# A decoder block in f32: the norm's sums of squares taken from turned x by one-column products, and a product moved ahead

## The chip, the cores and the metric

The kernel runs on one core of one Trainium2 chip. The metric is the device time of one execution in microseconds (us); the times of the kernel before are 1396.84, 1398.39 and 1398.48, median 1398.39. All arithmetic is f32. Each core has five engines that run side by side and meet through semaphores: PE (TensorE, matmuls; PEld is its weight load), DVE (VectorE), ACT (ScalarE), POOL (GpSimd), and SP, which here issues every transfer.

## The reference

A decoder block over x of shape (16, 256, 512), 4096 tokens of 512 channels. It has three parts, each with a residual and a layer norm behind it. What matters here is the beginning of the first:

```
xn   = x * rsqrt(mean(x*x, axis=-1) + EPS) * w_norm
proj = einsum('bld,td->blt', xn, W_in)          # z, xi, dt, B, C
xi   = silu(causal_conv4(xi))
...                                             # a scan over time with dA, u, C
y    = einsum('blh,ih->bli', y, W_h2i) * silu(z)
out  = einsum('bli,di->bld', y, W_out) + residual
x    = layernorm(x + out)
...                                             # long convolution with skip, contraction
...                                             # feed-forward with gated LoRA experts
```

## The kernel before, in words

The first part works on 8 groups of 512 tokens (`GT`), the other two on 32 slices of 8 time steps. The order of instructions on every engine is the order in which the program writes them; nothing is reordered by a scheduler, so a product that waits holds up all products behind it.

For a group the kernel needs x twice. `xnT` holds it turned, channels on partitions: four chunks `kc` of 128 channels by 512 tokens, which is what the projections multiply. `xt` holds it with tokens on partitions, four tiles of 128 tokens by 512 channels; it is the residual, added at the end of the group (L855). In the kernel before, the `xt` tiles also give the norm. `rms` (L404) squares each tile with an accumulated sum along the row (ACT L415, DVE L411), adds the epsilon (L417) and takes the power -1/2 on POOL (L419). That gives one number for each token, on partitions. `along_tokens` (L422) turns such numbers into rows that are equal on all partitions, by a product with the identity (L425), and `normed` (L444) multiplies `xnT` by them and by the norm's weight `wn` (L446). For the first group `rms` and `along_tokens` run in two halves of 256 tokens. Later groups take their rows through DRAM.

The projections use a scheme with seven products in place of eight for a block of 2 by 2 (`Xs`): four blocks of the turned x ("11", "12", "21", "22"), four sums of blocks `T1` to `T4` (L251, L254, L255, L257), and for each pair of weight blocks four weight sums `S1` to `S4` (`weight_sums`, L261 to L264, on POOL). A call of `product` (L356) is two matmuls of 256 columns. `begin_products` makes the block product A11 by "11", `first_products` three more: S1 by `T1`, S2 by `T2`, S3 by `T3`; the last three follow one step later. For the very first pair of the first group the second pair's `begin_products` is put between its T1 and T2 products, through the argument `between`:

```
if between is not None:
    between()
product(al[:, S:], w, p, S2, "T2", stop=True)
product(be[:, S:], w, p, S3, "T3", stop=True)
```

TensorE also multiplies the identity by itself at the start, for no result: `idle(n)` (L517) issues n such products of 128 columns, eight at first (`WARM`), then four after each half of the norm.

Transfers are issued by SP in program order. At the start these are: the four tiles `xt` (256 KB each), `wn`, the first half of `xnT` (512 KB), the first pair of `w_xi`, the second half of `xnT`, further weights (512 KB for a pair), small vectors, the rest of `w_z`, `w_bc`, then `w_h` and `w_o`. A transfer can wait until the one eight places before it has landed.

Of the kernel before, what the change touches and what calls it, by code (L numbers as in the profile page):

```python
# [8 lines left out]
F32 = mybir.dt.float32  # L9
# [5 lines left out]
P = 128  # L15
# [58 lines left out]
def decoder_kernel(  # L74
# [135 lines left out]
    with ExitStack() as s1:  # L210
# [12 lines left out]
        def load_x(g):  # L223
            xs = []
            for t in range(TT):
                xt = xp.tile([P, D], F32, tag="xt", name="xt")
                nc.sync.dma_start(xt, xg[g * TT + t])
                xs.append(xt)
            return xs
# [34 lines left out]
            eng.tensor_tensor(w[:, p, S4], w[:, p, A12], w[:, p, S2], ALU.subtract)  # L264
            return ins

        xs_next = load_x(0)
        wn = wp.tile([P, KD], F32, name="wn")
        nc.sync.dma_start(wn, w_norm)
        w_xi = big.tile([P, NI // 2, 7, 2, P], F32, tag="big", name="w_xi")  # L270
        w_z = big.tile([P, NI // 2, 7, 2, P], F32, tag="big", name="w_z")
        nc.sync.dma_start(xnT[:, 0:2], xTg[:, 0:2, 0:GT])
        nc.sync.dma_start(w_xi[:, 0, 0:4], Wxi[:, 0])
        nc.sync.dma_start(xnT[:, 2:4], xTg[:, 2:4, 0:GT])
        nc.sync.dma_start(w_xi[:, 1, 0:4], Wxi[:, 1])
        nc.sync.dma_start(w_z[:, 0, 0:4], Wz[:, 0])
        for p in range(2, NI // 2):
# [11 lines left out]
            nc.sync.dma_start(w_z[:, p, 0:4], Wz[:, p])  # L289
        w_bc = w1.tile([P, 2, 7, 2, P], F32, name="w_bc")  # L290
        nc.sync.dma_start(w_bc[:, :, 0:4], Wbc)


        w_h = w1.tile([P, 2, 2, P], F32, name="w_h")
# [69 lines left out]
                    skip_group_check=upon,  # L364
                )

        def begin_products(w, p, third):

            al, be = [
                ps_s.tile([P, 512], F32, tag="s", name="s") if third else bank() for _ in range(2)  # L370
            ]
            product(al[:, 0:S], w, p, A11, "11", start=True)
            return al, be

        def first_products(w, p, third, begun=None, between=None):

            al, be = begun or begin_products(w, p, third)
            product(be[:, 0:S], w, p, S1, "T1", start=True)
            if between is not None:
                between()  # L380
            product(al[:, S:], w, p, S2, "T2", stop=True)
            product(be[:, S:], w, p, S3, "T3", stop=True)
            return al, be
# [17 lines left out]
            nc.vector.tensor_tensor(to[1], u, be[:, 0:S], ALU.add)  # L401
            nc.vector.tensor_tensor(to[2], u, be[:, S:], ALU.add)

        def rms(xs, both=False):  # L404

            n = len(xs)
            ss = p2.tile([P, TT], F32, tag="ss", name="ss")[:, 0:n]
            for t in range(n):
                sq = p2.tile([P, D], F32, tag="acc", name="sq", bufs=6)
                if both and t % 2:  # L410
                    nc.vector.scalar_tensor_tensor(  # L411
                        sq, xs[t], 1.0, xs[t], ALU.mult, ALU.mult, accum_out=ss[:, t : t + 1]
                    )
                else:
                    nc.scalar.activation(sq, xs[t], AF.Square, accum_out=ss[:, t : t + 1])  # L415
            ms = p2.tile([P, TT], F32, tag="ms", name="ms")[:, 0:n]
            nc.vector.tensor_scalar(ms, ss, 1.0 / D, RMS_EPS, ALU.mult, ALU.add)  # L417
            rstd = p2.tile([P, TT], F32, tag="rstd", name="rstd")[:, 0:n]
            nc.gpsimd.tensor_tensor(rstd, ms, nhalf[:, 0:n], ALU.pow)  # L419
            return rstd  # L420

        def along_tokens(ps, rstd):  # L422

            for t in range(2):
                nc.tensor.matmul(  # L425
                    ps[:, t * P : (t + 1) * P],
                    rstd[:, t : t + 1].to_broadcast([P, P]),
                    ident,
                    start=True,
                    stop=True,  # L430
                )
# [85 lines left out]
        def idle(n):  # L517

            ps = bank()
            for _ in range(n):  # L520
                nc.tensor.matmul(ps[:, 0:P], ident, ident, start=True, stop=True)


        rt = ps_t.tile([P, GT], F32, tag="tr", name="rt")
        idle(WARM)
        for b in range(GB):
            along_tokens(
                rt[:, b * S : (b + 1) * S], rms(xs_next[b * TT // GB : (b + 1) * TT // GB], True)
            )
            idle(WARM // 2)  # L530
        normed(rt, (0, 1))
        first_token_sum(nc.vector)
        normed(rt, (2, 3))
# [54 lines left out]
        for g in range(groups):  # L588
# [97 lines left out]
            for i, (kind, p) in enumerate(order):  # L686
                if g == 1 and i == 2:
                    with_identity(w_f)
                if g in (2, 3) and i == 5:
                    w, cols = ((w_f, D), (w_gl, NG))[g - 2]  # L690
                    sums.append((w, cols, chunk_sum(w, cols)))
                if i == 6:
                    ms = [head_means(0)]
                if g == 0 and i == 0:
                    al, be = first_products(
                        kinds[kind], p, True, None,
                        lambda: begun.append(begin_products(w_xi, order[1][1], False)),
                    )
                else:
                    al, be = first_products(  # L700
                        kinds[kind], p, i % 3 == 0, begun.pop(0) if begun else None
                    )
                if i == 8:
                    ms.append(head_means(1))
                if i == 9:


                    yps = ps_t.tile([P, S], F32, tag="tr", name="yps")
                    for ht in range(HT):
                        for b in range(GB):  # L710
                            nc.tensor.matmul(
                                yps[b * HP : (b + 1) * HP],
                                sel[:, ht].rearrange("p q h -> p (q h)"),
                                Bs[ht][:, b * S : (b + 1) * S],
                                start=(ht == 0),
                                stop=(ht == HT - 1),
                            )
                    if sums:
                        centred(*sums.pop(0))
                if before is not None:  # L720
                    finish_products()
                to = places(kind, p)
                u = first_sums(al, be, to)
                if i == 8:
                    states(1, stepped(ms[1], spreads[2]), spreads[3])
                if i == 6:
                    ms = [stepped(ms[0], spreads[0])]
                    spreads.append(spread(1, 1))
                if g == 0:
                    if i == 1:  # L730
                        parts = decays()
                    if i == 2:
                        nc.scalar.activation(A, A, AF.Exp)
                        nc.vector.tensor_scalar(A, A, -1.0, None, ALU.mult)
                    if i in (1, 2, 4):
                        next(parts)
                if i == 9:
                    yT = q3.tile([P, S], F32, tag="vn", name="yT", bufs=1)
                    nc.scalar.copy(yT, yps)
                if before is not None:  # L740
                    finish_sums((lambda: next(parts)) if g == 0 and i == 2 else None)
                if g == 0 and i == 3:
                    next(parts)
                if g == 0 and i in later:
                    for n, (w, k) in enumerate(later[i]):
                        ins = weight_sums(nc.gpsimd, w, k)
                        if n == 0:
                            wait_for(ins, mixes[-1])
                if i == 7:
                    states(0, ms[0], spreads[1])  # L750
                if i == 8:
                    outputs(0)
                    outputs(1)
                    if more:
                        rt = to_dram(rms(xs_next))
                    if g == 0:
                        behind = []
                        w_sums = w_o_sums(behind)
                        next(w_sums)
                before = (kind, p, al, be, u, to)  # L760
                if g:
                    if i in (2, 5):
                        for one in turning[:2]:
                            turned(g - 1, *one)
                        del turning[:2]
                    if i in (0, 2):
                        t, r = late[i // 2]
                        late[i // 2] = t, r, spreads_of(r)
                    if i in (1, 3):
                        normalised(g - 1, *late[i // 2])  # L770
                        turning.append(late[i // 2][:2])
                if i == (6 if g else 1) and more:
                    xs_next = load_x(g + 1)
# [995 lines left out]
```

## Time and profile before

| | |
|---|---|
| median of three runs | 1398.39 us |
| profiled execution | 1399.62 us |
| its span, first to last instruction | 1397.8 us |
| PE busy | 1379.8 us, 99% of the span |
| DVE busy | 1186.5 us, 85% |
| POOL busy | 620.2 us, 44% |
| ACT busy | 450.2 us, 32% |

The profile is of one execution. The sections show busy time by engine, the span in slices, the chain of work that ended last, and groups of instructions; a line as L425 is a line of the kernel before. A f32 matmul appears as two records, each with its weight load. In a timeline a row is start, length, engine, line, operation, output and inputs, the number of records merged, and in brackets the idle time ahead of it with what ended it. Busy time of TensorE counts records, which overlap, so it is not a measure of how much of its peak is used.

### The profile page before, as it was taken

The numbers are of one execution on the slowest core, as the hardware profiler recorded it, in microseconds if no ns is written. First come the engines' busy times: TensorE is split into PE (matmuls) and PEld (weight loads), VectorE is DVE, ScalarE is ACT, GpSimd is POOL, SyncE is SP. The second block draws the span as 40 slices with busy tenths as digits, with TensorE's granted clock in tenths as the row PEclk, the third lists the DMA queues.
The fourth block names the chain that finished last, engine by engine and source line by source line (L and its number), as shares of the span: only waits on it lengthen the run. The fifth ranks groups of instructions, "written<-read, shape, count | busy, mean of one in ns | idle before, by whom it ended". The sixth has DMA issues, their size and how long they took to land.

```text
span 1397.8 us, 19582 instructions
## 1 busy us (share of the span) xinstructions
PE 1379.8 (99%) x6967; PEld 935.3 (67%) x6967; DVE 1186.5 (85%) x2270; ACT 450.2 (32%) x979; POOL 620.2 (44%) x849
## 2 busy tenths in 40 slices
PE   8999999999999999999999999999999999999997
PEld 7888788788888887888886345445454454545444
DVE  6888879878788787788866889999999999999986
ACT  2524324243243342432421323333323333333232
POOL 5451021020100201001003768877888788887884
PEclk9999999999999999999999999999999999999999
DMA  8113212212113131121306554454543555345500
GB/s 307 34 38 91 63 54 37 69 40 55 39 41 68 49 68 39 41 53 42 80 20 87 69 69 64 60 74 61 76 64 60 74 76 76 61 61 72 65 27 38
DMA packets 362386, 89.48 MB, mean 64 GB/s; under 512 B 330032, under 2 KB 334512, under 8 KB 362288
## 3 DMA queue, kind: packets, MB, share of 16 engines
q1 hardware_dynamic: 362288, 88.23, 34.1%
q8 instruction: 55, 0.90, 0.3%
q14 instruction: 43, 0.35, 0.1%
HBM read 70.62 MB, written 17.58 MB: 63 GB/s over the span
## 4 chain that ended last, share of the span: by engine, by line
PE 94%; DVE 3%; issue 1%; DMA 1%; POOL 0%; ACT 0%; SPq 0%; POOLq 0%; DVEq 0%
PE mm L358 21%; PE y L1088 15%; PE s L358 14%; PE y L1103 12%; PE s L826 6%; PE mm L826 6%; PE y L1070 4%; PE be L1335 4%; PE al L1335 3%; PE gl L1280 2%; PE xm L634 1%; PE mm L783 1%; PE mm L920 1%; PE al L1307 1%; PE s L920 1%
## 5 line engine op out<-in xcount | busy, mean ns | idle before, releaser
L1136 DVE TENSOR_TENSOR pr<-y,cT 128x1024 f32<-128x1024 f32 x126 | 148.4, 1219 | 38.4 <-PE y L1103 37.7
L1103 PE MATMUL y<-kv 64*64 64x512 f32 x1536 | 179.6, 598 | 0.0
L187 DVE TENSOR_TENSOR kv<-tr,cT 128x1024 f32<-128x1024 f32 x128 | 150.0, 1212 | 0.8 <-ACT tr L179 0.8
L623 DVE SCALAR_TENSOR_TENSOR acc<-xi,wc,acc 128x512 f32<-128x512 f32 x192 | 142.8, 757 | 7.4 <-ACT acc L619 1.8
L1146 DVE TENSOR_REDUCE red<-pr 128x128 f32<-128x1024 f32 x126 | 147.1, 1208 | 0.0
L1088 PE MATMUL y<-kv 128*128 128x512 f32 x272 | 128.3, 594 | 3.5 <-DVE pr L1136 3.4
L1103 PEld LDWEIGHTS y<-kv 64*64 64x64 f32 x1536 | 52.2, 132 | 118.6 <-issue 96.7
L69 POOL TENSOR_TENSOR rs_a<-ve_a,nhalf 128x1 f32<-128x1 f32 x32 | 17.5, 546 | 255.3 <-DVE ve_a L67 255.0
L1088 PE MATMUL y<-kv,Td 128*128 128x512 f32 x248 | 116.5, 592 | 0.0
L419 POOL TENSOR_TENSOR rstd<-ms,nhalf 128x4 f32<-128x4 f32 (+1 forms) x9 | 8.6, 954 | 229.7 <-DVE ms L417 229.7
L358 PE MATMUL mm<-XT,w_z 128*128 128x256 f32 x384 | 90.7, 379 | 0.0
L1088 PEld LDWEIGHTS y<-kv,Td 128*128 128x128 f32 x248 | 47.1, 190 | 59.3 <-issue 59.3
L1077 ACT COPY y<-y 64x512 f32<-64x512 f32 x120 | 67.0, 558 | 59.5 <-PE y L1070 57.6
L1088 PEld LDWEIGHTS y<-kv 128*128 128x128 f32 x272 | 51.1, 189 | 44.9 <-ACT y L1077 17.3
L1054 POOL TENSOR_TENSOR xs<-kv 128x512 f32<-128x512 f32 x63 | 80.2, 1273 | 0.1
L358 PEld LDWEIGHTS mm<-XT,w_z 128*128 128x128 f32 x384 | 73.0, 190 | 9.9
L358 PE MATMUL mm<-xnT,w_z 128*128 128x256 f32 x288 | 70.8, 382 | 0.0
L1490 POOL TENSOR_TENSOR ol<-o,red 128x512 f32<-128x512 f32 x31 | 39.3, 1267 | 61.4 <-DVE red L1146 61.4
L251 POOL TENSOR_TENSOR XT<-xnT 128x512 f32<-128x512 f32 x7 | 9.3, 1326 | 129.0 <-PE mm L826 129.0
L1070 PE MATMUL y<-xs,kv 128*128 128x512 f32 x120 | 62.2, 600 | 0.4
L358 PE MATMUL s<-XT,w_xi 128*128 128x256 f32 x256 | 61.0, 380 | 0.8 <-DVE XT L254 0.5
L358 PEld LDWEIGHTS mm<-xnT,w_z 128*128 128x128 f32 x288 | 54.0, 190 | 10.1 <-issue 3.0
(337 smaller groups left out, 3065.6 us busy)
## 6 DMA issues: line engine op xcount, KB each, us to landing
cT<-in_ctxT SPq DMA_DIRECT2D x32, 384.0 KB
kv<-in_toep SPq DMA_DIRECT2D x32, 384.0 KB
xt<-in_x SPq DMA_DIRECT2D x32, 256.0 KB
spread<-both SPq DMA_DIRECT2D x32, 256.0 KB
first<-xt SPq DMA_DIRECT2D x124, 64.0 KB
vT<-first SPq DMA_DIRECT2D x31, 256.0 KB
out<-res SPq DMA_DIRECT2D x31, 256.0 KB
xnT<-in_xT SPq DMA_DIRECT2D x7, 1024.0 KB
```

The costliest lines, as they stand in the source:

```text
L187: last = nc.vector.tensor_tensor(kv[:, q, k * BQ : (k + NL // 2) * BQ], vT[:, q, blks].rearrange("p k (b i) -> p (k b) i", i=NH).unsqueeze ...
L358: nc.tensor.matmul(ps, w[:, p, a, kc, :], Xs[b][:, kc, :], start=start and kc == 0, stop=stop and kc == 1, skip_group_check=upon,)
L623: ins = nc.vector.scalar_tensor_tensor(acc, xi[:, :, k : k + S], wc[:, c, k : k + 1], acc, ALU.mult, ALU.add)
L826: nc.tensor.matmul(ps, own[a][c][:, n * P : (n + 1) * P], w_o[b][c], start=start and c == 0, stop=stop and c == HC - 1, skip_group_check=upon,
L1054: return nc.gpsimd.tensor_tensor(xs[:, q], moving(kv, q, 0), moving(kv, q, 1), ALU.add)
L1070: nc.tensor.matmul(seed, T[:, SHARED_AT, :], xs[:, q], start=True, stop=True)
L1077: nc.scalar.copy(bank_of(y, 2)[b : b + HP], seed[a : a + HP])
L1088: nc.tensor.matmul(bank_of(y, lb), w, moving(kv, q, mb), start=not late and lb not in begun, stop=False, skip_group_check=True,)
L1103: return nc.tensor.matmul(bank_of(y, lb)[cols], T[rows, DIAGONAL_AT, (b - a) * HP : (b - a + 1) * HP], moving(kv, q, lb)[rows], start=star ...
L1136: nc.vector.tensor_tensor(pr.rearrange("p (k b j) i -> p k b j i", k=2, j=NH), y[i].rearrange("p k (b j i) -> p k b j i", j=NH, i=NH), cT[ ...
L1146: nc.vector.tensor_reduce(red[:, q, 2 * i : 2 * i + 2, :].rearrange("p k t -> p (k t)"), pr, AX.X, ALU.add)
L1335: nc.tensor.matmul(ps, a[:, kc, :], w[:, kc, :], start=(start and kc == 0), stop=(kc == 1), skip_group_check=True,)
```

## The change

Four things change, all in the first group.

The transfers: both halves of `xnT` are now issued first, then `wn`, then the weights as before; the four tiles `xt` of the first group are issued after `w_bc`, ahead of `w_h` and `w_o`.

The norm of the first group: a new function `rms_from_columns` squares the four chunks of `xnT` (two on ACT, two on DVE) and sums over channels on TensorE. For each chunk and each 128 tokens the squared block is the stationary operand and one column of -1/2 (`nhalf`) the moving one, sixteen products of one column, accumulated in one bank. `inverse`, the former end of `rms`, scales by -2/D. `idle(WARM // 4)`, two products, stands after chunks 0 and 2.

The spreading along tokens: one call with four products in place of two calls with two. `idle` runs four products ahead of it and four behind it.

The products: for the second pair, both the A11 product and the S1 by T1 product now stand in front of the first pair's T2 product; before, only A11 did. The order on TensorE up to there, before and after (s is the first pair, mm the second):

```
before  s 11 | s T1 | mm 11 | s T2 | s T3 | mm T1 | mm T2 | mm T3
after   s 11 | s T1 | mm 11 | mm T1 | s T2 | s T3 | mm T2 | mm T3
```

The diff, cut to its core:

```diff
-        xs_next = load_x(0)
         wn = wp.tile([P, KD], F32, name="wn")
-        nc.sync.dma_start(wn, w_norm)
...
         nc.sync.dma_start(xnT[:, 0:2], xTg[:, 0:2, 0:GT])
+        nc.sync.dma_start(xnT[:, 2:4], xTg[:, 2:4, 0:GT])
+        nc.sync.dma_start(wn, w_norm)
         nc.sync.dma_start(w_xi[:, 0, 0:4], Wxi[:, 0])
-        nc.sync.dma_start(xnT[:, 2:4], xTg[:, 2:4, 0:GT])
...
         nc.sync.dma_start(w_bc[:, :, 0:4], Wbc)
+        xs_next = load_x(0)
...
-        def begin_products(w, p, third):
+        def begin_products(w, p, third, second=False):
...
             product(al[:, 0:S], w, p, A11, "11", start=True)
+            if second:
+                product(be[:, 0:S], w, p, S1, "T1", start=True)
             return al, be
...
-            al, be = begun or begin_products(w, p, third)
-            product(be[:, 0:S], w, p, S1, "T1", start=True)
+            al, be = begun or begin_products(w, p, third, True)
...
+        def rms_from_columns(ps, between):
+
+            for kc in range(KD):
+                sq = p2.tile([P, GT], F32, tag="acc", name="sq", bufs=6)
+                if kc % 2:
+                    nc.vector.tensor_tensor(sq, xnT[:, kc, :], xnT[:, kc, :], ALU.mult)
+                else:
+                    nc.scalar.activation(sq, xnT[:, kc, :], AF.Square)
+                for t in range(TT):
+                    nc.tensor.matmul(
+                        ps[:, t : t + 1],
+                        sq[:, t * P : (t + 1) * P],
+                        nhalf[:, 0:1],
+                        start=(kc == 0 and t == 0),
+                        stop=(kc == KD - 1),
+                        skip_group_check=True,
+                    )
+                if kc % 2 == 0:
+                    between()
+            return inverse(ps[:, 0:TT], -2.0)
...
         def along_tokens(ps, rstd):
-            for t in range(2):
+            for t in range(TT):
...
+        ss = ps_t.tile([P, TT], F32, tag="tr", name="ss")
         rt = ps_t.tile([P, GT], F32, tag="tr", name="rt")
         idle(WARM)
-        for b in range(GB):
-            along_tokens(
-                rt[:, b * S : (b + 1) * S], rms(xs_next[b * TT // GB : (b + 1) * TT // GB], True)
-            )
-            idle(WARM // 2)
+        rstd = rms_from_columns(ss, lambda: idle(WARM // 4))
+        idle(WARM // 2)
+        along_tokens(rt, rstd)
+        idle(WARM // 2)
         normed(rt, (0, 1))
...
-                        lambda: begun.append(begin_products(w_xi, order[1][1], False)),
+                        lambda: begun.append(begin_products(w_xi, order[1][1], False, True)),
```

## The prediction

> **What bounds the kernel now.** I read the page's busy shares first, then busy time by stretch, then the chain of waits over the first 60 us, then the timeline of the first 20 us engine by engine.
>
> ```profile
> PE 1379.8 (99%) x6967; PEld 935.3 (67%) x6967; DVE 1186.5 (85%) x2270; ACT 450.2 (32%) x979; POOL 620.2 (44%) x849
> ...
> 0.00:17.40 17.40, 13.65 (x60) 11.16 (x61) 9.43 (x18) 3.10 (x6) 9.85 (x26) 1.00 0.92 323
> 17.40:130.00 112.60, 112.60 (x603) 94.37 (x603) 95.75 (x204) 42.08 (x82) 45.51 (x73) 1.00 0.32 95
> ```
>
> The columns after the length are busy PE, PEld, DVE, ACT and POOL, then clock, DMA share and GB/s. From 17.40 to 130 us TensorE has no idle time at all. So whatever moment its unbroken run begins, and however much matmul work is still left then, passes one for one to the end. Every edit lies ahead of that moment. What sets it is read in the chain (start, length, what):
>
> ```profile
> 2.10 5.76 DMA xt<-in_x
> ...
> 7.88 0.71 DVE sq L411 x2
> ...
> 8.69 0.18 DVE ms L417
> ...
> 8.94 0.72 POOL rstd L419
> ...
> 9.70 0.78 PE rt L425 x4
> ...
> 10.51 1.42 DVE xnT L446 x2
> ...
> 14.06 1.17 DVE XT L254
> ...
> 15.37 1.10 PE s L358 x4
> ```
>
> So the start is a latency chain: x lands, is squared, the root is taken and spread over partitions, then VectorE scales xnT at 10.51 and makes the token sums. Call that moment N. The products then wait for VectorE. TensorE's own timeline:
>
> ```profile
> 6.28 1.22 PE L425 MATMUL rt<-ident,rstd 128*128 128x128 f32 x4 [0.68 <-POOL rstd L419]
> 7.29 1.91 PE L521 MATMUL mm<-ident 128*128 128x128 f32 x8
> 9.70 0.76 PE L425 MATMUL rt<-ident,rstd 128*128 128x128 f32 x4 [0.50 <-POOL rstd L419]
> 10.30 1.06 PE L521 MATMUL mm<-ident 128*128 128x128 f32 x8
> ...
> 13.79 1.03 PE L358 MATMUL mm<-xnT,w_xi 128*128 128x256 f32 x4
> 15.37 2.23 PE L358 MATMUL s<-XT,w_xi 128*128 128x256 f32 x8 [0.54 <-DVE XT L254]
> ```
>
> Two things are to be seen. A f32 matmul leaves two records. And eight identical warm-up records take 1.91 us at 7.29, but 1.06 at 10.30. With the last one's own length taken off (0.42 and 0.28 us), one record starts each 0.213 us early and each 0.112 us late: TensorE runs at half pace until about 9.8 us. The page's granted-clock row reads 9 there and does not show it; the pitch does.
>
> **The change part by part.**
>
> *The reorder of the second pair's T1 product.* In the old order TensorE finishes that pair's first product and idles 0.54 us for T2, then runs s T2 and waits for T3 (ready 16.35, start 16.47); the second pair's T1 product comes after, from 17.43. In the new order it stands in the gap. One product is two matmuls, four records; twelve records take 2.59 us in the chain, so four take 0.86. From 14.65 it would run to 15.51, so s T2 starts 0.14 later than before, and s T3 still starts by T3, at N+5.96. All 0.86 us then leaves the queue behind it: **-0.86**. Its operand S1 of the second pair must be ready: POOL's fifth weight sum, which ended at 14.67, just in time. In the new kernel POOL starts its weight sums after the only root, about 1.4 us ahead of N instead of 0.12 behind it, so it is earlier where it counts.
>
> *SP's order.* xnT is first, wn next, then the weights; x goes behind w_bc. Each issue costs SP 0.43 us. wn passes two queue places and is not read before N. The weights gain 1 MB of head start, and w_xi (POOL waited for it 0.98 us until 10.63) stops being late. x, now ahead of w_h and w_o, delays those by its 1 MB, some 3 us at 350 GB/s; w_o is first read at 73.8, w_h at 76.0, x at 95.0, and the DMA rows fall to near nothing by 34 us. **0**; the cover is over 30 us. xnT itself lands like x did: x's four tiles are used at 3.77, 4.43, 7.23 and 7.88, so the first half of xnT (the bytes of two tiles) at about 4.4, the second at 6 to 7.9.
>
> *Squares.* Before: two on ACT, two on DVE, each with a read of its sum (0.19, 0.08). After: the same four without that read, but over channels. ACT 0.63, DVE 0.69 to 0.77. The first pair is done at 5.1 to 5.2, the second at 7 to 8.6. No cost by itself.
>
> *Sixteen one-column products.* This is the new work on the path: 32 records, in line with two pairs of warm-up products (8 records). No row shows a one-column matmul. Bounds: each needs a whole 128x128 load. The nearest row is the warm-up, where the second load ends 0.215 us after the first at half pace, and 0.112 at full pace, with the stream of 128 columns taking the same. So 0.213 and 0.111 a record is the upper end. The Trainium skill, "TensorE: Matmul & The Clock Gate", section "LDWEIGHTS (loading the stationary operand)", speaks against the edit as well, since a load's time goes by the weight's columns, however few columns stream past; but it gives P/1.2, 107 ns for 128. By that rule at half pace (and half of it, 0.056, at full) 32 records cost 1.8 to 3.4 us, by the row 3.6 to 6.8. I take the row: it is measured, f32, at both paces.
>
> TensorE is free for them at 5.38 (the first warm-up's last record starts at 5.17). The 40 records up to the last column then depend on when full pace comes. Before it came at 9.84, over gaps of 0.68 and 0.50 us. The same page, section "Part 1: The HAM clock gate (the 'warmup' mystery)", says that one busy window of 3.4 us, free-running, lifts the gate: with TensorE busy from 1.80 on without a gap, that is between 5.2 and 8.6. The trace asks for caution: from 1.80 to 9.70 it stayed at half pace though TensorE was idle for only 1.18 of 7.9 us. Middle, 6.9: by then 7.1 records are done; the first 20 end at 8.33, the third chunk waits for its square until 8.6 if xnT lands late, and 20 more at 0.111 end at 10.80. With 5.4: 9.8. With 9.84: 12.0.
>
> *From the columns to N.* Result 0.15 (estimate, half of a record's latency), ms 0.22, root on POOL 0.81, then four products to spread it instead of two, since the second half no longer comes alone: 0.76 for two at full pace, plus four records of 0.111, 1.21; hand-overs 0.10. Sum 2.49. N becomes 10.80+2.49 = 13.29, against 10.51: **+2.78** (5.4: +1.8; 9.84: +3.9). What is queued behind these waits: on VectorE the scalings, on POOL the weight sums, 1.2 us later in absolute time, earlier against N; both are in the sum.
>
> Together +2.78-0.86 = **+1.9 us**, with ends +0.9 (full pace at 5.4) and +3.0 (at 9.84). The profiled execution took 1399.62 (span 1397.8, 1.8 around it), 1.2 over the median 1398.39; the difference is applied to the median: 1400.3.
>
> **The rivals.**
>
> *The one-column products do not count as activity and TensorE stays at half pace (slower).* Its place is the stretch 5.4 to 16: one column moves through the array for each 128 loaded, and the only dense stretches are warm-ups of 0.85 us. For it: 85% of records in flight had not been enough until 9.84 before. Against: its loads and records follow one another without a gap. Price: 40 records of 0.213 end at 13.9, the last result 14.15, root at 15.2, behind it four warm-ups until 15.6, spreading at half pace at first until 17.1: N later by 6.6, less 0.86, +5.7: 1404.1. It decides from where full pace comes after about 9.5 us; between, +3.
>
> *A cheap column (equal or faster).* Loads at the rule's 0.107 and 0.056, full pace at 6.9, xnT at 6: the columns end at 8.8, N at 11.3, net -0.1; with xnT at 8.6, +1.1; with full pace at 5.4, 8.1 and -0.8. For it: the rule, and a load that might pass when almost nothing streams. Against: consecutive loads end 0.112 apart in the trace. About 1398.4, from 1397.6 to 1399.5.
>
> *The reorder does not do what it says.* If S1 of the second pair comes after T2, the product waits in front of T2 instead of behind T3 and its 0.86 is lost: +2.8, 1401.2. Against: POOL's start, above.
>
> **How the numbers follow.** Forecast 0.57, half pace 0.25, cheap column 0.14, lost reorder 0.04. 0.2% is 2.8 us, about what a measurement of this kernel can tell from no change. Over it on the slow side: all of the half-pace case, a sixth of the forecast (late full pace) and half of the lost reorder: 0.37. On the fast side no sum reaches -2.8; 0.02 is left for what I have not seen. Within: 0.61. The range from 1398.0 to 1404.3 takes in the cheap column's middle and the half-pace sum. The forecast's own is 1399.3 to 1401.4.
>
> **What would show it.** The first scaling of xnT (10.51 before) near 13.3; column records about 0.11 to 0.21 us apart; no wait for T2 ahead of s T2, and an unbroken run after it; x landed long before 95 us. Wrong, if the columns come faster than 0.1 us a record and N is below 11.4 (then it is faster), or if warm-up records behind the columns still stand 0.213 apart (then it is the half-pace case).

## The result, and the profile after

The changed kernel takes 1403.05 us at the median (8 runs, 1401.24 to 1404.81), the kernel before 1398.43 (8 runs). The ratio is 1.0031, interval [1.0022, 1.0041]: slower by 4.6 us. The forecast was 1400.3 in a range to 1404.3. The median hides two levels. Four runs lie between 1401.24 and 1401.64, with a mean TensorE clock of 0.995 or 0.996; four lie between 1404.46 and 1404.81, with 0.998 or 0.999; no run lies at the median. The profiled execution, 1404.81 us and a span of 1403.0, is one of the upper level.

Its TensorE timeline over the start (start, length, operation, output and inputs, records merged; the brackets give the idle time ahead):

```profile
5.49 1.87 PE L431 MATMUL ss<-nhalf,sq 128*128 128x1 f32 x8
7.22 1.20 PE L542 MATMUL mm<-ident 128*128 128x128 f32 x4
8.21 3.41 PE L431 MATMUL ss<-nhalf,sq 128*128 128x1 f32 x16
11.49 1.20 PE L542 MATMUL mm<-ident 128*128 128x128 f32 x4
12.48 1.71 PE L431 MATMUL ss<-nhalf,sq 128*128 128x1 f32 x8
14.05 2.06 PE L542 MATMUL mm<-ident 128*128 128x128 f32 x8
15.89 1.87 PE L446 MATMUL rt<-ident,rstd 128*128 128x128 f32 x8
17.60 1.06 PE L542 MATMUL mm<-ident 128*128 128x128 f32 x8
```

TensorE is never idle here, and yet nothing gets faster until 17.6 us. Sixteen one-column records take 3.41 us and start 0.213 apart; the eight warm-ups at 14.05 take 2.06 us and the eight at 17.60 only 1.06. Half pace, which ended at 9.8 us in the profile of the kernel before, lasts to 17.6. The chain of waits over the same stretch (start, length, what) is all TensorE up to the scaling of xnT:

```profile
5.59 1.77 PE ss L431 x8
7.36 1.06 PE mm L542 x4
8.42 3.20 PE ss L431 x16
11.63 1.06 PE mm L542 x4
12.69 1.50 PE ss L431 x8
14.19 1.92 PE mm L542 x8
16.10 1.68 PE rt L446 x8
...
17.87 1.42 DVE xnT L467 x2
19.28 0.02 issue
19.31 1.11 DVE XT L251
...
20.55 1.10 PE s L358 x4
21.65 1.73 PE mm L358 x8
23.38 1.86 PE s L358 x8
25.23 1.73 PE mm L358 x8
26.96 2.59 PE s L358 x12
```

The first scaling of xnT starts at 17.87 instead of 10.51, 7.36 later. The new order gives part of it back: no wait stands between 20.55 and 26.96, where the chain before had one for T2. The product group that the chain before started at 20.19 starts at 26.96, 6.77 later; from there the shift is carried through the first part of the kernel. The spans differ by less, 5.2 us. In this one pair of executions SP took 0.25 us instead of 0.97 for one issue at the turn to the second part, and the last instructions came 0.7 sooner after the rest. No edit touches either; why they differ is open.

### The profile page after: what moved, and what is told of

Same layout as the page of the kernel before. It is cut to its first block, busy times and chain, and to the rows that moved or that the text cites. A ratio compares the mean times of both kernels' runs of the same rounds, so it can differ in the third digit from the quotient of the medians.

```text
span 1403.0 us, 19650 instructions
## 1 busy us (share of the span) xinstructions
PE 1387.8 (99%) x7007; PEld 944.5 (67%) x7007; DVE 1186.7 (85%) x2267; ACT 450.2 (32%) x977; POOL 620.3 (44%) x848
## 4 chain that ended last, share of the span: by engine, by line
PE 95%; DVE 3%; issue 1%; POOL 0%; ACT 0%; DMA 0%; SPq 0%; POOLq 0%; DVEq 0%
PE mm L358 21%; PE y L1109 15%; PE s L358 14%; PE y L1124 12%; PE s L847 6%; PE mm L847 6%; PE y L1091 4%; PE be L1356 4%; PE al L1356 3%; PE gl L1301 2%; PE xm L655 1%; PE mm L804 1%; PE mm L941 1%; PE al L1328 1%; PE s L941 1%
## 5 line engine op out<-in xcount | busy, mean ns | idle before, releaser
L411 POOL TENSOR_TENSOR rstd<-ms,nhalf 128x4 f32<-128x4 f32 x8 | 8.2, 1027 | 236.0 <-DVE ms L409 236.0
```

## The experiments

**Is it the width of the products?** The sixteen products are kept in number, place and load, but stream 128 equal columns (the tile `ss` grows to hold them):

```diff
-                        ps[:, t : t + 1],
+                        ps[:, t * P : (t + 1) * P],
                         sq[:, t * P : (t + 1) * P],
-                        nhalf[:, 0:1],
+                        nhalf[:, 0:1].to_broadcast([P, P]),
...
-            return inverse(ps[:, 0:TT], -2.0)
+            return inverse(ps[:, 0 : TT * P : P], -2.0)
```

> The changed kernel with its sixteen products 128 columns wide (the same column of -1/2 repeated), one of the 128 equal result columns used; same number of instructions, loads and records. Theory A (the clock gate looks at how much streams through the array, so one-column products leave it closed): the products keep their pitch of 0.213 us at first, full pace comes between 5 and 9 us, the first scaling of xnT starts near 13 instead of 17.9, and the time is 1399.5 to 1401. Theory B (the gate looks at instructions in flight, and the changed kernel stays at half pace for another reason, as the place of its windows): as the changed kernel, first scaling near 17.5, 1403. Theory C (the cost is the load, whatever the pace): as the changed kernel too, or a little more.

Measured: 1399.69 us (13 runs, 1398.86 to 1400.37), kernel before 1397.98 on the same chip; ratio 1.0012, [1.0003, 1.0020]. Its TensorE timeline:

```profile
5.36 1.06 PE L431 MATMUL ss<-nhalf,sq 128*128 128x128 f32 x8
6.25 0.61 PE L542 MATMUL mm<-ident 128*128 128x128 f32 x4
6.70 1.95 PE L431 MATMUL ss<-nhalf,sq 128*128 128x128 f32 x16
8.48 0.61 PE L542 MATMUL mm<-ident 128*128 128x128 f32 x4
8.93 1.06 PE L431 MATMUL ss<-nhalf,sq 128*128 128x128 f32 x8
```

The same sixteen records now take 1.95 us instead of 3.41, with 128 times as many columns. Full pace is there from 5.3 us on, and the first scaling starts at 12.62. More streaming made the kernel 3.4 us faster at the median, or 2.9 when each is measured against its own runs of the kernel before. All 13 times lie below the lower level of the changed kernel, so a lucky place of the gate's windows in one profile is not the reason. Theory A stands; B and C, which expected the changed kernel's time, fall. With the columns the results written and the multiplications grow too; no run here separates these.

**What width holds the gate?** Sixty-four extra products of the identity in the middle of groups 1 to 5 of the kernel before, at full pace, of five widths:

```diff
+PROBE = {1: 1, 2: 16, 3: 32, 4: 64, 5: 128}
...
+        def probe(width):
+            ps = bank()
+            for _ in range(64):
+                nc.tensor.matmul(
+                    ps[:, 0:width], ident, ident[:, 0:width], start=True, stop=True
+                )
...
+                if g in PROBE and i == 3:
+                    probe(PROBE[g])
```

> The kernel before with 64 extra products of the identity in the middle of groups 1 to 5, at full pace: 1 column wide in group 1, then 16, 32, 64, 128. Theory A: in the 1-column stretch the pitch goes from about 0.11 to about 0.21 us a record within 3.4 to 7 us, and the first products after it run at half pace for some us; at 128 columns it stays at 0.11; somewhere between lies the width that holds. That adds 5 x 14 us at full pace, about 9 us more for each stretch that falls to half pace. Theory B: 0.11 in all five stretches. Theory C adds: no column count below 128 goes under 0.11; a cheap column (rival of the prediction) would show a pitch of 0.06 or less in the 1-column stretch.

Measured: 1504.59 us (one execution, in which each width ran once, in a group of its own). Busy time and granted clock by stretch in its trace (start and end, length, busy PE, PEld, DVE, ACT, POOL, then the clock, the DMA share, GB/s). The one-column stretch begins at 121.0, the 16-column one at 238.8, the 32-column one at 359.5, those of 64 and 128 at 475.8 and 582.0:

```profile
120.00:125.00 5.00, 5.00 (x43) 4.87 (x41) 4.83 (x16) 2.00 (x4) 0.00 (x0) 1.00 0.01 4
125.00:130.00 5.00, 5.00 (x28) 5.00 (x28) 0.98 (x4) 0.00 (x0) 0.81 (x2) 0.56 0.69 107
130.00:150.00 20.00, 20.00 (x82) 18.87 (x83) 0.05 (x1) 0.37 (x1) 0.00 (x0) 0.51 0.00 1
...
230.00:270.00 40.00, 40.00 (x188) 37.68 (x187) 11.27 (x24) 6.33 (x11) 4.82 (x6) 0.66 0.11 22
330.00:380.00 50.00, 50.00 (x283) 46.14 (x281) 25.41 (x61) 13.43 (x21) 9.57 (x15) 0.85 0.12 29
440.00:480.00 40.00, 40.00 (x232) 35.38 (x231) 30.70 (x73) 13.80 (x22) 7.49 (x10) 1.00 0.11 32
560.00:610.00 50.00, 50.00 (x295) 45.74 (x294) 28.92 (x67) 14.80 (x26) 3.24 (x8) 1.00 0.13 29
```

PE is busy in every one of these stretches from end to end. The clock nevertheless falls to one half in the first three and stays at 1.00 with 64 and 128 columns, whose products take 14.4 us each. The half-pace stretches last 23.9, 27.3 and 20.5 us; the rows of 16 and 32 columns are means over longer stretches, 0.66 with 27.3 of 40 us at half, 0.85 because the row ends at 380 and half pace at 385. The length of the run bears this out: five times 14.4 us and half of 71.7 at half pace are 108 us (an estimate from these figures), and the run is 106.6 longer than the kernel before. A record of 1 to 128 columns starts every 0.112 us at full pace, and every 0.213 us at half pace. So a one-column product is not cheaper than a 128-column one. What is left to set the pitch is the load, since issuing can be faster: in the kernel before 32 records with loads of 32 columns take 1.08 us.

```profile
22.71 1.08 PE L460 MATMUL d_lg<-xnT,w_dt 128*32 128x128 f32 x32
```

In the one-column case the products end at 144.0 and full pace returns only at 149.5: dense work has to go on for some time first.

**The two levels.** The changed kernel again, unaltered: seven runs together, then two single ones.

> The changed kernel once more, unaltered, for its two levels (four of eight times near 1401.4, four near 1404.5). If they come from the place of the gate's free-running windows, the profile of this run is in one of two forms: full pace from about 17 us as before and a time near 1404.5; or full pace early, between 5 and 6.5 us, lost again about 3.4 us later in the one-column stretch, and back before the first products, with a time near 1401.4 and a mean clock of 0.995 to 0.996. If they come from elsewhere, both levels show the same start.

Measured: seven runs, four at 1401.37 to 1401.82 (clock 0.996) and three at 1404.37 to 1404.67 (0.998, 0.999). Its profile was of the upper level again, with full pace from 17.35.

> The changed kernel unaltered, one profile, for the lower of its two levels, which no profile has shown so far. If the place of the gate's windows makes the levels: either full pace only from about 17 us and 1404.5, or full pace early (5 to 6.5 us), half pace again about 3.4 us later inside the one-column products, full pace before the first products, a first scaling of xnT about 3 us earlier than 17.7, and 1401.5.

Measured: 1404.35, the upper level, as before.

> As the look before it: the other form of the start, should that one have shown the known form again.

Measured: 1401.34, mean clock 0.996. Here is the lower level, first by stretch (columns as above), then on TensorE:

```profile
6.00:8.00 2.00, 2.00 (x19) 2.00 (x20) 0.64 (x1) 0.57 (x1) 0.00 (x0) 1.00 0.94 340
8.00:10.00 2.00, 2.00 (x18) 2.00 (x17) 0.00 (x0) 0.00 (x0) 0.00 (x0) 0.86 1.05 371
10.00:12.00 2.00, 2.00 (x11) 2.00 (x11) 0.16 (x1) 0.00 (x0) 0.83 (x1) 0.50 1.02 408
...
7.09 1.84 PE L431 MATMUL ss<-nhalf,sq 128*128 128x1 f32 x16
8.79 0.69 PE L542 MATMUL mm<-ident 128*128 128x128 f32 x4
9.32 1.57 PE L431 MATMUL ss<-nhalf,sq 128*128 128x1 f32 x8
10.75 2.06 PE L542 MATMUL mm<-ident 128*128 128x128 f32 x8
```

The gate opened at 6.04, behind the dense warm-ups, closed at 9.46 amid the one-column products, and opened again at 16.28. In between the records of the two middle chunks ran at full pace (sixteen in 1.84 us), with the warm-ups around them; the rest ran at half pace. The first scaling started at 14.61, 3.26 before that of the profile above; the distance of the levels is 3.1 us. So the early opening makes the lower level. That it comes or not by where the gate's windows fall is worked out from the times: openings and closings lie 3.41 us or whole multiples of it apart (9.46 less 6.04; 16.28 less 9.46 is 6.83). Counted back in such steps from the opening at 17.6, windows of the upper level's profile end at 3.9 and 7.4 and hold 2.1 and 1.6 us of the first warm-ups, which run from 1.8 to 5.5; the window that ends at 6.04 holds 2.8 us of them (estimates). This fits; no run moved the windows by intent.

**What is the new order worth?** The changed kernel with the old order:

```diff
-            al, be = begun or begin_products(w, p, third, True)
+            al, be = begun or begin_products(w, p, third)
+            product(be[:, 0:S], w, p, S1, "T1", start=True)
...
-                        lambda: begun.append(begin_products(w_xi, order[1][1], False, True)),
+                        lambda: begun.append(begin_products(w_xi, order[1][1], False)),
```

> The changed kernel with the old product order. The gain of the order, 0.7 us, is lost: 1403.7, with its two levels near 1402.1 and 1405.2 if the two levels of the changed kernel come from the place of the gate's windows. If the order does nothing behind the late start, 1403.0.

Measured: 1402.28, 1402.36, 1402.40 (clock 0.996) and 1404.72, 1405.40 (0.999, 0.998), against 1401.2 to 1401.8 and 1404.4 to 1404.8. In the lower level the order is worth about 0.9 us; in the upper one two runs are too few to tell (0.25 and 0.9 above the middle of the others). And alone, in the kernel before (the lines of the change that deal with `second`):

> The kernel before with the product order alone (the second pair's S1 by T1 product in front of the first pair's T2 product). All theories: one product of 0.86 us fills the 0.54 us gap; the shift of 7.36 us at the first scaling of xnT that the changed kernel shows has become 6.65 after the first products, so 0.7 us of gain is expected: 1397.7, between 0.4 and 0.9 below the kernel before. If the gain was only an effect of the other edits (POOL's earlier weight sums), nothing: 1398.4.

Measured: 1398.39 (13 runs) against 1397.98 (25 runs), ratio 1.0000, [0.9992, 1.0008]. No gain shows, though an interval of 1.1 us to each side would hide one of 0.86. TensorE and POOL in its profile:

```profile
12.23 1.13 PE L358 MATMUL mm<-xnT,w_xi 128*128 128x256 f32 x4
14.24 1.13 PE L358 MATMUL mm<-XT,w_xi 128*128 128x256 f32 x4 [0.88 <-POOL w_xi L261]
...
9.66 0.73 POOL L261 TENSOR_TENSOR w_xi<-w_xi 128x256 f32<-128x256 f32 x1 [1.50 <-DMA w_xi<-in_Wxi]
10.47 1.22 POOL L262 TENSOR_TENSOR w_xi<-w_xi 128x256 f32<-128x256 f32 x1
11.65 0.73 POOL L263 TENSOR_TENSOR w_xi<-w_xi 128x256 f32<-128x256 f32 x1
12.33 0.73 POOL L264 TENSOR_TENSOR w_xi<-w_xi 128x256 f32<-128x256 f32 x1
13.02 1.17 POOL L261 TENSOR_TENSOR w_xi<-w_xi 128x256 f32<-128x256 f32 x1
```

Here the first scaling starts at 8.97, because the third and fourth tile of x came sooner than in the first profile (the last squares start at 6.40 instead of 7.88). POOL's chain of weight sums moves less, by 1.0 us (from 10.63 to 9.66) where the scaling moves 1.5: it hangs on the landing of w_xi. So the moved product waits 0.88 us for the fifth sum, and stands in front of T2's product while it does. The wait for T2 has become a wait for POOL.

**Mending both.** First, the wide products without the four warm-ups between them (`rms_from_columns(ss, lambda: None)` in the wide kernel):

> The changed kernel with products 128 columns wide and without the two pairs of warm-up products between them (8 records). If the chain of products on TensorE sets the first scaling of xnT once the gate is open, it starts 0.9 us earlier than the 12.62 of the wide kernel, at 11.7, and the time is 0.9 less, near 1398.8. If xnT's arrival sets it, it stays at 12.6 and 1399.7.

Measured: 1398.48 (13 runs), ratio 1.0001, [0.9992, 1.0009]; first scaling at 11.96. The 32 records now run in one piece, 5.38 to 9.34, the first scaling comes 0.66 sooner, and the time falls by 1.2. With the gate open the chain of products and of the root behind them sets the start, and this way of taking the norm is as fast as the old one within 1.3 us.

Second, the kernel before with the new order, and on POOL the second pair's first sum ahead of the first pair's last:

```diff
-        for w, p in ((w_xi, 0), (w_xi, 1), (w_z, 0), (w_xi, 2)):
-            weight_sums(nc.gpsimd, w, p)
+        two = [weight_sums_of(nc.gpsimd, w_xi, p) for p in range(2)]
+        for n in (0, 0, 0, 1, 0, 1, 1, 1):
+            next(two[n])
+        for w, p in ((w_z, 0), (w_xi, 2)):
+            weight_sums(nc.gpsimd, w, p)
```

(`weight_sums_of` makes the same four sums one at a time.)

> The kernel before with the new product order, and the second pair's first weight sum on POOL moved ahead of the first pair's last one. With the new order alone TensorE waited 0.88 us for that sum (from 13.1 to 14.24). If this wait is what took the order's gain, it goes: the sum follows the second pair's landing at 12.2 and ends near 13.1, TensorE runs unbroken from about 12.2, and the time is 0.7 to 1.2 below the kernel before, near 1397.0. If the order gains nothing in any case, 1398.0.

Measured: 1398.31 (13 runs) against 1398.28 (43 runs), ratio 0.9999, [0.9990, 1.0007]. The wait is gone from its profile (the moved product starts at 14.11, right behind the one at 13.14), yet the median does not show it (the interval is again 1.4 us below to 1.0 above). Three of its times lie at 1399.5 to 1400.3 with a clock of 0.997, as eight of the kernel before lie at 1399.86 and above; no profile shows this level. Third, the same with `idle(WARM + 2)` at first:

> As the one with the changed order of sums, and ten warm-up products at first instead of eight, which fill the gap of 0.5 to 0.7 us ahead of the first spreading. If the upper level of the kernel before (1399.3 to 1400.0, a fifth of its times, mean clock 0.997) comes from a window that this gap leaves too empty, that level is gone and the median falls by 0.3 to 0.5 more; otherwise the same as without, or up to 0.4 later where the two products stand in the way.

Measured: 1397.44 (21 runs, 1396.58 to 1398.33), ratio 0.9992, [0.9986, 0.9999]. That upper level does not appear in 21 runs, and this version is ahead of the kernel before, if by 0.8 us only. The two warm-ups were not run without the new orders, so their share is open.

## Why the prediction was right, and where not

*Sign and size.* Slower, as forecast, and inside the range, but not for the reason given. The forecast's own stretch, 1399.3 to 1401.4, was missed, and so was what the text held most likely, a time within 0.2% of the old one (0.61). The range held the result because it was drawn out to the half-pace rival (1404.1), and by luck: half of the eight runs lie at 1404.5, above the range, half at 1401.4, and 1403.05 is a point between them. With five in the upper level the median would have been out. By the text's own sign, warm-ups behind the columns still 0.213 us apart, both levels are the half-pace case.

*The step that failed is the moment of full pace.* The text took 6.9 us from the rule that a busy window of 3.4 us lifts the gate, and counted the one-column products as busy. They neither opened the gate nor held it open. Full pace came at 17.6 in one form; in the other it came at 6.04, within the span of 5.2 to 8.6 given, and was lost again after 3.41 us. Nor is 9.84 a fixed moment of the old norm: with the order alone full pace came at 5.3, with the order of sums at 8.0. On the page "TensorE: Matmul & The Clock Gate" the section "Part 1: The HAM clock gate (the 'warmup' mystery)" of the Trainium skill has the window's length right (3.41 in the trace), but its "busy" is not the profile's busy PE, which was 100% in stretches in which the clock fell.

*The rest of the sum.* With products that keep the gate open, the wide kernel has its first scaling at 12.62 and is 1.7 us slower than the kernel before. That is near the forecast's 13.29 and 1.9 in part by chance, since its gate opened at 5.3, and for a gate at 5.4 the sum gave 12.3 and 0.9. Of the 0.3 missing there, 0.2 is the root, which took 1.03 us on four columns, not the 0.81 put for it. The rival's sum put N, the first scaling, later by 6.6; it was 7.36. The columns ended at 14.19, not 13.9, and the sixteen records behind them took 3.6 us to 17.78, where the sum had 3.2: the spreading ran at half pace to its end. The slower root held nothing up here, since it was done at 15.50 and the warm-ups ran until 15.9.

*Load against stream.* The row was preferred to the rule: 0.213 us a record at half pace, 0.112 at full. The one-column records took exactly that. The rule's 107 ns fits the full pace alone, the half of it that the text took for full pace showed nowhere, and the cheap-column rival is refuted.

*The reorder.* Forecast -0.86; in the profiled pair it was 7.36 less 6.77, 0.59. What is missing is nearly all in the product on T3: it started 6.23 behind the first scaling, not 5.96, because the T1 sum, the first of the token sums on VectorE, took 1.10 us instead of 0.77. POOL's weight sums ran beside it in both profiles; why it took longer is open. The rival that S1 comes late was set aside for the changed kernel, and rightly there: it is the old kernel in which the order meets it, and shows no gain.

*SP's order* cost nothing: xnT was used at 4.81 and 6.12, POOL waited for no weights, and no wait for x, w_h or w_o appears in the chain of the first 60 us.

## What to carry to other kernels

In f32, with loads of 128 columns, a reduction by products with one column costs as much TensorE time as one with 128, and at the start of a kernel it costs more, since it does not open the clock gate: let filler or work that is to hold the gate stream at least 64 columns for each load. A move on one engine pays only if what it reads is ready on the others; look for the latest of all its inputs before and after, not only for the one whose wait is to be filled. Where times fall into two levels, a mean clock that moves with them points to the gate. Read it with the trace, though: here the slower level shows the higher mean, because its half pace ahead of the first opening is not in the figure. And the figure of the kernel before includes 5.5 us at half behind its last product, which cost nothing.

## What the runs showed of the hardware

The clock gate follows what streams. Back to back at full pace, f32 products of 1, 16 and 32 columns on 128-column loads closed it within 2.9 to 5.1 us, 64 and 128 did not in 14.4. At equal pitch a 32-column product streams a quarter of the time of a 128-column one, and a 64-column product half (an estimate from the widths), so the limit for these f32 products lies between the two. Once closed, it stayed so for 6.8 us in the lower level and for 20.5 to 27.3 us in the probe, of which the last 3.0 to 5.7 us were dense products of 256 columns behind the probe's own. The granted clock reads 1.00 ahead of the first event of a trace, also where the pitch shows half pace. So it stands in the upper level's profile (columns as above), in a stretch in which records start 0.213 us apart:

```profile
10.00:12.00 2.00, 2.00 (x10) 2.00 (x11) 0.00 (x0) 0.00 (x0) 0.00 (x0) 1.00 1.02 415
```

Early in an execution the pitch of equal records tells the pace, the clock row does not.
